# Later steps, row buffers taken twice and own PSUM banks in the projection stages of an attention-and-FFN kernel

## The chip, the core and the metric

The kernel runs on one core of a Trainium2 chip. The core has a matrix engine (TensorE, PE in the profile), a vector engine (VectorE, DVE), a scalar engine (ScalarE, ACT), a general engine (GpSimd, POOL) and a sync engine (SyncE, SP) that here does nothing but issue DMAs. Each engine runs its own instructions in the order of the program and waits on semaphores for the others. The metric is the device time of one execution in microseconds; lower is better. The kernel before takes 2465.11 us (median of 3 runs, 2461.74 to 2465.53).

## What is computed

Eight sequences of 512 rows and 1024 columns in float32 go through one transformer block without learned norms:

```python
x = x + _layernorm(attn(_layernorm(x), Wq, Wk, Wv, Wo))
x = x + _layernorm(ffn(_layernorm(x), weight, bias, lora_A, lora_B, lora_start_indices))
```

`attn` is causal attention with 16 heads of 64 and rotary positions, and ends with a product by `Wo`. `ffn` is one product by a 1024 x 1024 weight plus bias, and for most sequences a rank-16 LoRA term. So each sequence has two large 512 x 1024 by 1024 x 1024 products behind the attention, each followed by a layernorm over rows and an addition of the row that went in. In this text these are the projections: 0 to 7 are by `Wo` (one per sequence), 8 to 15 by the FFN weight.

## The kernel before

The program has three parts: the value projections with the layernorm of the input, then scores and attention, and last the sixteen projections. Only the last part changes, and in it mainly projections 0 to 7. It starts 1.67 ms into the span.

A projection is a Strassen-Winograd product, twice nested: 7 groups (`GROUPS`, order P1, P2, P4, P5, P7, P6, P3) of 7 products each (`SLOTS`, order P6, P1, P3, P5, P4, P7, P2). One product is two 128 x 128 by 128 x 256 matmuls, four records in the profile. So a projection is 49 products, and the program counts them: tick `49*q + 7*g + p` is product p of group g of projection q. `run(tick, filler)` issues the product, then the adds that drain the product before it, then whatever `at(tick, ...)` has put on that tick. Ticks only set the order in each engine's queue; no engine waits for a tick.

A group has four PSUM accumulators. a and b take two products each and have two buffers. c and d are the two halves of one 2 KB bank, also with two buffers; c takes P5 and, two products into the next group, P3, and d takes P4. `Group.drain` empties them: after P1, ACT copies a to `p1` and DVE makes `u2 = p1 + b`; after P7, DVE adds b into `p1` and writes `p1 + d` and `p1 + c` to the result; after P2, ACT copies a out; after P3, DVE writes `c + u2`. Three of these are waits for PE: P7 adds into b, so it waits for `u2`; P3 adds into c, so it waits until the drain after P7 has read c; P2 adds into a, so it waits for the copy to `p1`.

The seven group results are combined by 128 x 1024 additions: on DVE `c11 += A` (tick 18), `U += A` (45), `c22 += U` (46), `c12 += c22` (48), `c22 += A` (52), and on POOL in two halves `c21 += c12` (38), `c21 += U` (47) (line 360). The right operands of the next projection are R11, R21, R12, R22, loaded by SP at ticks 10, 17, 24, 31, and differences T1, T2, T4, T3 of them, which POOL makes at ticks 38, 45, 52 and 63 in three instructions each (line 274). They are written into buffers of the projection that is running: T1 takes the one that held R12, or rather T3, which overwrites R12 in place. T3 is the right operand of group P7, whose last product (P3) is at tick 37.

While projection q+1 runs, the four row tiles t of projection q are finished (`plan_rows`). A row tile is 128 rows by 1024 columns in two halves. For projections 0 to 7 the steps are: load the row of the input (SP), statistics (two `bn_stats`, `bn_aggr`, a square root on ACT, then reciprocal and bias on DVE; key `o`), normalise (two ACT instructions), add the row (two POOL instructions, line 1158), store to `x1`, statistics again (key `x`), normalise into the row's buffer (ACT), transpose in 32 x 32 blocks back into the result's place (two DVE instructions, line 1167), store to `x1t` (eight DMAs, line 1174). Tile t begins at tick `k = 55 + 7*t` of projection q, that is `6 + 7*t` of the next. The row's buffer is held from the load to the transposes; three buffers rotate and one tile of each projection takes a fourth.

Projections 8 to 15 load their right operands from `x1t` (four DMAs each, line 254), take differences of them on POOL and DVE (line 262), have T1 and T3 made by DVE, and have two small LoRA products (line 1187) at ticks 25 and 39 of the projection before. Their row tiles stop after the first addition.

Of the kernel before, what the change touches and what calls it, by code (L numbers as in the profile page):

```python
# [10 lines left out]
F32 = mybir.dt.float32  # L11
# [6 lines left out]
P = 128  # L18
B, S, E = 8, 512, 1024
# [44 lines left out]
SUB = 256  # L64
# [68 lines left out]
def sandwich_kernel(  # L133
# [58 lines left out]
    def at(tick, fn, kind=None):  # L192
        events[tick].append((kind, fn) if kind else fn)
# [100 lines left out]
    class Group:  # L294
# [9 lines left out]
        def product(self, p):  # L304
            l, r, a = SUBS[p]
            first = a not in self.acc
            if a in "ab" and first:
                self.acc[a] = env["acc"].tile([P, SUB], F32, tag=a, bufs=2, name=f"acc{a}_{self.name}")
            elif a == "c" and first:
                both = env["acc"].tile([P, 2, SUB], F32, tag="c", bufs=2, name=f"accc_{self.name}")  # L310
                self.acc["c"], self.acc["d"] = both[:, 0], both[:, 1]
            acc = self.acc[a]
            left, right = self.W[self.L], RX[self.q, self.R][:, SLOT_R[r]]
            for k in range(2):
                stays = right[:, k, :] if self.q < B else by_blocks(right, k)
                if self.q < 0:
                    moving = left[:, SLOT_L[l], k, :]
                else:
                    moving = left[:, 4 * k : 4 * k + 4, SLOT_L[l], :]
                nc.tensor.matmul(  # L320
                    acc, lhsT=stays, rhs=moving,
                    start=(first and k == 0), stop=True, skip_group_check=True,
                )
            if self.lora and p in LORA_SUB:
                half, cols = self.lora
                i, c = LORA_SUB[p]
                nc.tensor.matmul(  # L327
                    acc, lhsT=hts[self.q - B][:, cols[c], :],
                    rhs=env["lb"][self.q - B][:, half * HALF + i * SUB : half * HALF + (i + 1) * SUB],
                    start=False, stop=True, skip_group_check=True,  # L330
                )
# [7 lines left out]
        def drain(self, p):  # L339

            acc, t = self.acc, self.t
            add = lambda out, x, a: nc.vector.tensor_tensor(out, acc[a], x, op=ALU.add)
            if p == "P1":
                env["u2"].reverse()
                for n, pool in (("p1", env["p1"]), ("u2", env["u2"][0])):
                    t[n] = pool.tile([P, SUB], F32, tag=n, name=f"{n}_{self.name}")
                nc.scalar.copy(t["p1"], acc["a"])  # L347
                add(t["u2"], t["p1"], "b")
            elif p == "P7":
                add(t["p1"], t["p1"], "b")  # L350
                add(self.dest(1, 0), t["p1"], "d")
                add(self.dest(1, 1), t["p1"], "c")
            elif p == "P2":
                nc.scalar.copy(self.dest(0, 0), acc["a"])
            elif p == "P3":
                add(self.dest(0, 1), t["u2"], "c")
# [38 lines left out]
    def stats(key, srcs, step):  # L395
        small = env["small"]
        if step == 0:
            ln[key] = small.tile([P, 2, 6], F32, tag="bnst", name=f"bn_{key}")
        if step < 2:
            nc.vector.bn_stats(ln[key][:, step, :], srcs[step])  # L400
        if step == 1:
            mv = small.tile([P, 2], F32, tag="mv", name=f"mv_{key}")
            nc.vector.bn_aggr(mv, ln[key])
            ln[key] = mv
        if step == 2:
            mv = ln[key]
            sd = small.tile([P, 1], F32, tag="sd", name=f"sd_{key}")
            nc.scalar.activation(sd, mv[:, 1:2], AF.Sqrt, bias=eps, scale=1.0)
            ln[key] = mv, sd
        if step == 3:  # L410
            mv, sd = ln[key]
            rs = small.tile([P, 1], F32, tag="rstd", name=f"rstd_{key}")
            nc.vector.reciprocal(rs, sd)
            nb = small.tile([P, 1], F32, tag="nb", name=f"nb_{key}")
            nc.vector.tensor_scalar(nb, mv[:, 0:1], rs, -1.0, op0=ALU.mult, op1=ALU.mult)
            ln[key] = rs, nb
# [683 lines left out]
    with ExitStack() as a:  # L1100
# [23 lines left out]
        def pick_b(b):  # L1124
            lb[b] = (rows if b % 2 else lc).tile([P, E], F32, tag="lb", bufs=1, name=f"lb_{b}")
            pick(lb[b], lora_b, 1, b)
# [12 lines left out]
        def halves(q, t):  # L1139
            h, j = divmod(t, 2)  # L1140
            tags = (("c11", "c21"), ("c12", "c22") if q + 1 == NQ else ("c22", "c12"))[h]
            return [C[q, tag][:, j, :] for tag in tags]

        row = {}

        def load_row(q, t):
            if (q, t) == (NQ - 1, 3):
                row[q, t] = lc.tile([P, E], F32, tag="lb", bufs=1, name=f"row_{q}_{t}")
            elif q < B and t == (3 if q + 1 < B else 0):
                row[q, t] = rows.tile([P, E], F32, tag="lb", bufs=1, name=f"row_{q}_{t}")  # L1150
            else:
                row[q, t] = rows.tile([P, E], F32, tag="row", bufs=3, name=f"row_{q}_{t}")
            src = x[q, ts(t, P), :] if q < B else x1d[q - B][:, t, :]
            nc.sync.dma_start(out=row[q, t], in_=src)

# [45 lines left out]
        def plan_right(q, base):  # L1201

            if q > 1:
                at(base + 6, next_roles)
            for n, k in (("R11", 10), ("R21", 17), ("R12", 24), ("R22", 31)):
                if q == 1 and n != "R22":
                    continue
                at(base + k, lambda n=n: load_right(gp, q, n))
                if q >= B:
                    at(base + k + 4, lambda n=n: sub_right(q, n, nc.gpsimd, slice(0, 3)))  # L1210
            if q >= B:
                for h, k in ((0, 25), (1, 39)):
                    at(base + k, lambda h=h: lora_in(q - B, h), "pe")
                    at(base + k, lambda ph, h=h: lora_keep(q - B, h, ph), "post")
                    for g in range(2):
                        at(base + k, lambda n=f"R{g + 1}{h + 1}": sub_right(q, n, nc.vector if h else nc.gpsimd, slice(3, 4)))
                at(base + 42, lambda: sub_ht(q - B))
                if q - B:
                    at(base + (10 if q - B > 1 else 33), lambda: pick_b(q - B))
                if q + 1 < NQ:  # L1220
                    at(base + 43, lambda: pick_a(q - B + 1))
            for n, k in (("T1", 40 if q == 1 or q >= B else 38), ("T2", 46 if q >= B else 45), ("T4", 52), ("T3", 63)):
                eng = nc.vector if q >= B and n in ("T1", "T3") else nc.gpsimd
                for m in range(3):
                    at(
                        base + k + (m if eng is nc.vector else 0),
                        lambda n=n, m=m, eng=eng: sum_right(gp, q, n, eng, slice(m, m + 1)),
                    )
# [8 lines left out]
        def plan_rows(q, base):  # L1237

            for t in range(NT):
                k = base + 55 + 7 * t  # L1240
                key = f"{'o' if q < B else 'y'}{q}_{t}"
                at(k, lambda t=t: load_row(q, t))
                for m in range(4):
                    at(k + m + m // 2, lambda t=t, m=m, key=key: stats(key, halves(q, t), m))
                for h in range(2):
                    at(k + 6 + h, lambda t=t, h=h, key=key: norm(key, halves(q, t)[h], halves(q, t)[h]))
                    at(k + 8 + h, lambda t=t, h=h: add_row(q, t, h))
                at(k + 14, lambda t=t: store_rows(q, t))
                if q < B:
                    key = f"x{q}_{t}"  # L1250
                    for m in range(4):
                        at(k + 14 + m + m // 2, lambda t=t, m=m, key=key: stats(key, halves(q, t), m))
                    for h in range(2):
                        at(k + 20 + h, lambda t=t, h=h, key=key: norm(
                            key, row[q, t][:, ts(h, HALF)], halves(q, t)[h]
                        ))
                    for g in range(2):
                        at(k + 24 + g, lambda t=t, g=g: turn_x1(q, t, g))
                        at(k + 29 + g, lambda t=t, g=g: store_x1(q, t, g))

        def plan_last(q, base):

# [169 lines left out]
```

## Time and profile before

The profiled execution took 2465.22 us, of which 2463.1 us are the profile's span. All times of places below are microseconds from the span's start.

| part of the span | us | PE busy | DVE busy | POOL busy |
|---|---|---|---|---|
| whole span | 2463.1 | 2352.0 | 1752.8 | 1535.6 |
| while projection 2 runs (1741.28 to 1786.27) | 44.99 | 42.72 | 40.17 | 36.80 |
| while projection 3 runs (1786.27 to 1831.29) | 45.02 | 42.73 | 40.23 | 36.87 |
| while projection 5 runs (1876.30 to 1922.80) | 46.50 | 44.25 | 40.17 | 36.03 |
| while projection 7 runs (1967.82 to 2023.45) | 55.63 | 46.76 | 48.75 | 46.67 |
| while projection 8 runs (2023.45 to 2085.11) | 61.66 | 54.87 | 50.30 | 41.71 |

A stretch is counted from the start of one product P3 at tick 2 to the next, because PE waits there in each of them. PE is the engine with least idle time, so a stretch is read as PE's busy time plus the waits that ended last. The order of the instructions is fixed on every engine, so a late instruction makes all behind it in its queue late too.

### The profile page before, as it was taken

The page shows a single profiled execution, that of the slowest core. Times are in us where ns is not written, and L with a number is a line of the kernel's source. Part 1 is how long each engine was busy: PE and PEld are TensorE (multiplying, and loading weights), DVE is VectorE, ACT ScalarE, POOL GpSimd, SP SyncE. Part 2 cuts the span into 40 slices and gives each one's busy share as a digit, 9 for nine tenths or more (in the row PEclk, how much of TensorE's full clock was granted, in tenths as well). Part 3 has the DMA queues.
Part 4 walks back from the last instruction along what each step waited for, and adds up shares of the span by engine and source line. Part 5 has one row for each costly group of instructions (what it writes and reads, how often), then busy time and mean ns, then how long its engine had stood idle before and what let it go on. Part 6 is the DMA issues. An engine that isn't in the chain of part 4 may idle for free.

```text
span 2463.1 us, 37159 instructions
## 1 busy us (share of the span) xinstructions
PE 2352.0 (95%) x11936; PEld 1857.2 (75%) x11936; DVE 1752.8 (71%) x3834; ACT 1110.5 (45%) x2790; POOL 1535.6 (62%) x1139
## 2 busy tenths in 40 slices
PE   6999999999999999999999999899999988999997
PEld 4888887877677777777777767458888867888886
DVE  8666566475857759586684866776888988777676
ACT  5445541126555555655555566652434333222223
POOL 4978774204463553736645364776886886777874
PEclk8999999999999999999999999999999999999999
DMA  7688887998899897989989896567777798455443
GB/s 277 201 289 263 252 277 250 331 289 270 261 298 281 248 343 238 320 295 291 327 262 333 265 307 232 145 240 262 231 208 241 208 267 237 139 144 146 136 122 120
DMA packets 506017, 606.48 MB, mean 246 GB/s; under 512 B 197600, under 2 KB 344032, under 8 KB 503264
## 3 DMA queue, kind: packets, MB, share of 16 engines
q1 hardware_dynamic: 504288, 598.87, 76.7%
q0 software_dynamic: 1536, 5.24, 0.7%
q8 instruction: 96, 1.57, 0.3%
q14 instruction: 97, 0.79, 0.1%
HBM read 371.20 MB, written 199.23 MB: 232 GB/s over the span
## 4 chain that ended last, share of the span: by engine, by line
PE 69%; DVE 7%; DMA 3%; ACT 2%; POOL 2%; SPq 1%; issue 1%; ACTq 0%; DVEq 0%; POOLq 0%
PE accc_P L320 10%; PE accc_q_P L675 7%; PE accb_q_P L675 7%; PE acca_q_P L675 7%; PE s L787 6%; PE accb_P L320 6%; PE acca_P L320 6%; PE po L869 6%; PE ptp L848 5%; PE accd_q_P L675 4%; DMA R<-x1t 1%; PE accc_P L327 1%; DVE U L360 1%; ACT pr L818 1%; DMA qk<-D_q 1%
## 5 line engine op out<-in xcount | busy, mean ns | idle before, releaser
L818 ACT ACTIVATE pr<-pr,nm 128x128 f32<-128x128 f32 (+3 forms) x512 | 281.0, 550 | 189.1 <-DVE nm L808 189.0
L834 ACT ACTIVATE pr<-pr,rs 128x128 f32<-128x128 f32 x470 | 231.0, 550 | 105.9 <-DVE rs L826 105.8
L808 DVE CUSTOM_DVE_ANT_0 pr<-s,mask 128x128 f32<-128x128 f32 (+3 forms) x512 | 224.5, 485 | 45.3 <-PE s L787 43.4
L675 PE MATMUL accc_q_P<-xs,ls 128*128 128x256 f32 x896 | 218.4, 387 | 0.0
L675 PE MATMUL acca_q_P<-xs,ls 128*128 128x256 f32 x896 | 217.3, 385 | 0.7 <-issue 0.7
L1158 POOL TENSOR_TENSOR c<-c,row 128x512 f32<-128x512 f32 x120 | 161.6, 1355 | 89.3 <-ACT c L450 83.1
L675 PE MATMUL accb_q_P<-xs,ls 128*128 128x256 f32 x896 | 216.3, 384 | 0.8 <-DVE u_q_P L116 0.8
L675 PEld LDWEIGHTS acca_q_P<-xs,ls 128*128 128x128 f32 x896 | 165.3, 190 | 49.8 <-issue 21.9
L675 PEld LDWEIGHTS accc_q_P<-xs,ls 128*128 128x128 f32 x896 | 166.2, 191 | 48.5 <-issue 22.5
L787 PE MATMUL s<-qk 64*128 64x128 f32 (+3 forms) x1024 | 194.7, 472 | 6.7 <-DVE nm L808 4.8
L675 PEld LDWEIGHTS accb_q_P<-xs,ls 128*128 128x128 f32 x896 | 165.4, 190 | 44.9 <-issue 7.7
L848 PE MATMUL ptp<-ident,pr 128*128 128x128 f32 x1280 | 177.6, 278 | 9.8 <-ACT pr L834 7.3
L601 POOL TENSOR_TENSOR wc_g<-wc_g 128x256 f32<-128x256 f32 (+1 forms) x120 | 130.2, 1103 | 79.5 <-DMA wc_g<-in_wqk_dram 76.2
L274 POOL TENSOR_TENSOR T<-R,T 128x512 f32<-128x512 f32 (+1 forms) x96 | 170.5, 1802 | 13.8 <-PE accc_P L320 9.6
L848 PEld LDWEIGHTS ptp<-ident,pr 128*128 128x128 f32 x1280 | 147.3, 142 | 40.6 <-ACT pr L834 11.2
L869 PE MATMUL po<-pT,v 128*64 128x384 f32 (+3 forms) x1024 | 156.3, 444 | 8.2 <-ACT pT L863 6.1
L869 PEld LDWEIGHTS po<-pT,v 128*64 128x64 f32 x1024 | 71.5, 138 | 100.4 <-issue 66.1
L718 POOL TENSOR_TENSOR B_q<-B_q,m 128x1024 f32<-128x1024 f32 x14 | 33.2, 2369 | 180.8 <-DVE B_q L715 180.7
L787 PEld LDWEIGHTS s<-qk 64*128 64x128 f32 x1024 | 73.6, 186 | 48.8 <-issue 28.9
L675 PE MATMUL accd_q_P<-xs,ls 128*128 128x256 f32 x448 | 108.8, 386 | 0.4 <-DVE p_q_P L116 0.4
L863 DVE COPY pT<-ptp 128x384 f32<-128x384 f32 (+1 forms) x132 | 80.5, 615 | 39.4 <-PE ptp L848 39.4
L347 ACT COPY p_P<-acca_P 128x256 f32<-128x256 f32 x109 | 40.5, 372 | 144.0 <-PE acca_P L320 107.5
(938 smaller groups left out, 5775.1 us busy)
## 6 DMA issues: line engine op xcount, KB each, us to landing
ls<-wqk SPq DMA_DIRECT2D x392, 256.0 KB, 5.0
xs<-xop SPq DMA_DIRECT2D x392, 256.0 KB, 5.2
R<-attn SPq DMA_DIRECT2D x32, 896.0 KB, 5.7
wqk<-wc_g SPq DMA_DIRECT2D x16, 1568.0 KB, 9.5
x<-in_x_dram SPq DMA_DIRECT2D x32, 512.0 KB, 9.8
v<-vd SPq DMA_DIRECT2D x64, 256.0 KB, 5.4
attn<-ops SPq DMA_DIRECT2D x16, 1024.0 KB, 7.7
row<-in_x_dram SPq DMA_DIRECT2D x32, 512.0 KB, 5.1
```

What stands on the lines that cost most here:

```text
L274: eng.tensor_tensor(RX[q, n][:, c], RX[q, x][:, c], RX[q, y][:, c], op=ALU.subtract)
L320: nc.tensor.matmul(acc, lhsT=stays, rhs=moving, start=(first and k == 0), stop=True, skip_group_check=True,)
L601: eng.tensor_tensor(out, x, y, op=op)
L675: nc.tensor.matmul(acc[:, :, w, :], lhsT=ls[:, k, w, :], rhs=xs_[:, :, k, :], start=(first and w == 0 and k == 0), stop=True, skip_group_c ...
L787: nc.tensor.matmul(ps[:, j, at : at + L], lhsT=qT[r, qb], rhs=kT[r, : qb + 1], start=True, stop=True,)
L808: nc.vector.tensor_tensor_reduce(out=v[:, j, :], in0=self.ps[qb][:, j, :], in1=work2["mask"][:, S - L :], scale=-1.0 / HD**0.5, scalar=3.0e38,
L818: nc.scalar.activation(v[:, j, :], v[:, j, :], AF.Exp, bias=nm[:, j : j + 1], scale=-1.0, accum_out=sm[:, j : j + 1],)
L834: nc.scalar.mul(v, v, rs[:, j : j + 1])
L848: nc.tensor.transpose(pt[:, n, :], self.pr[qb][:, j, ts(kb, P)], ident)
L863: copy(self.pT[j][:, : qb + 1, ts(qb, P)], self.pt[j][:, : qb + 1, :])
L869: nc.tensor.matmul(po[j * HD : (j + 1) * HD, kb * P :], lhsT=self.v[:, kb, ts(j, HD)], rhs=self.pT[j][:, kb, kb * P :], start=(kb == 0), s ...
L1158: nc.gpsimd.tensor_tensor(c, c, row[q, t][:, ts(h, HALF)], op=ALU.add)
```

## The change

Four things change in the projections; the number of instructions on every engine stays what it was, and so does what each computes.

- The two halves c and d of the shared bank become tiles of their own: c with two buffers, d with one. The drain after P7 reads c first and d second.
- In projections 0 to 7 the steps of a row tile are moved apart. Counted from k: the row's load from 0 to 5; statistics `o` from 0, 1, 3, 4 to 0, 1, 4, 6; the normalisation from 6 to 9; the addition of the row from 8 to 12; the store from 14 to 16; statistics `x` from 14, 15, 17, 18 to 16, 17, 20, 22; the second normalisation from 20 to 25.
- The transposes leave that grid. They were at 79, 86, 93 and 100 of projection q for the four tiles and are at 84, 91, 103 and 107. In the next projection's ticks: from 30, 37, 44, 51 to 35, 42, 54, 58, so those of the last two tiles stand behind the end of that projection. Their stores follow 5 ticks later as before.
- The row's buffer is taken twice: once for the loaded row, until it is added, and again (`open_row(..., True)`) for the second normalisation. Tile 2 (of projection 7 tile 0) takes the fourth buffer on the second occasion.

One gather of LoRA weights (`pick_b` for sequence 1) moves from tick 33 to 39 of projection 8, since it reuses that fourth buffer.

```diff
-            if a in "ab" and first:
-                self.acc[a] = env["acc"].tile([P, SUB], F32, tag=a, bufs=2, name=f"acc{a}_{self.name}")
+            if first and (a in "ab" or self.q >= 0):
+                self.acc[a] = env["acc"].tile(
+                    [P, SUB], F32, tag=a, bufs=1 if a == "d" else 2, name=f"acc{a}_{self.name}"
+                )
...
-                add(self.dest(1, 0), t["p1"], "d")
-                add(self.dest(1, 1), t["p1"], "c")
+                for half, a in ((0, "d"), (1, "c")) if self.q < 0 else ((1, "c"), (0, "d")):
+                    add(self.dest(1, half), t["p1"], a)
...
+        def open_row(q, t, turned=False):
+            if (q, t) == (NQ - 1, 3):
+                pool, tag, bufs = lc, "lb", 1
+            elif turned and t == (2 if q + 1 < B else 0):
+                pool, tag, bufs = rows, "lb", 1
+            else:
+                pool, tag, bufs = rows, "row", 3
+            row[q, t] = pool.tile([P, E], F32, tag=tag, bufs=bufs, name=f"row_{q}_{t}_{int(turned)}")
...
-                at(k, lambda t=t: load_row(q, t))
-                for m in range(4):
-                    at(k + m + m // 2, lambda t=t, m=m, key=key: stats(key, halves(q, t), m))
+                new = q < B
+                at(k + 5 * new, lambda t=t: load_row(q, t))
+                for m, n in enumerate((0, 1, 4, 6) if new else (0, 1, 3, 4)):
+                    at(k + n, lambda t=t, m=m, key=key: stats(key, halves(q, t), m))
                 for h in range(2):
-                    at(k + 6 + h, lambda t=t, h=h, key=key: norm(key, halves(q, t)[h], halves(q, t)[h]))
-                    at(k + 8 + h, lambda t=t, h=h: add_row(q, t, h))
-                at(k + 14, lambda t=t: store_rows(q, t))
-                if q < B:
+                    at(k + (9 if new else 6) + h, lambda t=t, h=h, key=key: norm(key, halves(q, t)[h], halves(q, t)[h]))
+                    at(k + (12 if new else 8) + h, lambda t=t, h=h: add_row(q, t, h))
+                at(k + (16 if new else 14), lambda t=t: store_rows(q, t))
+                if new:
                     key = f"x{q}_{t}"
-                    for m in range(4):
-                        at(k + 14 + m + m // 2, lambda t=t, m=m, key=key: stats(key, halves(q, t), m))
+                    for m, n in enumerate((16, 17, 20, 22)):
+                        at(k + n, lambda t=t, m=m, key=key: stats(key, halves(q, t), m))
+                    at(k + 25, lambda t=t: open_row(q, t, True))
                     for h in range(2):
-                        at(k + 20 + h, lambda t=t, h=h, key=key: norm(
+                        at(k + 25 + h, lambda t=t, h=h, key=key: norm(
                             key, row[q, t][:, ts(h, HALF)], halves(q, t)[h]
                         ))
+                    turn = base + (84, 91, 103, 107)[t]
                     for g in range(2):
-                        at(k + 24 + g, lambda t=t, g=g: turn_x1(q, t, g))
-                        at(k + 29 + g, lambda t=t, g=g: store_x1(q, t, g))
+                        at(turn + g, lambda t=t, g=g: turn_x1(q, t, g))
+                        at(turn + 5 + g, lambda t=t, g=g: store_x1(q, t, g))
```

More of the change, by code (lines that the diff above doesn't have):

```diff
@@ L1144, in sandwich_kernel @@
         row = {}
-        def load_row(q, t):
[L1147 to L1152, printed above, removed]
+        def open_row(q, t, turned=False):
[6 more added lines that the diff above has]
+            row[q, t] = pool.tile([P, E], F32, tag=tag, bufs=bufs, name=f"row_{q}_{t}_{int(turned)}")
+        def load_row(q, t):
+            open_row(q, t)
             src = x[q, ts(t, P), :] if q < B else x1d[q - B][:, t, :]
@@ L1218, in plan_right @@
                 if q - B:
-                    at(base + (10 if q - B > 1 else 33), lambda: pick_b(q - B))
+                    at(base + (10 if q - B > 1 else 39), lambda: pick_b(q - B))
                 if q + 1 < NQ:
```

## Prediction

> **What bounds the kernel now.** I read the page's engine shares first, then PE's waits in the part that changes, then the busy time of each stretch from one tick-2 wait to the next, then the three engines' instructions in order of time around one such wait.
>
> ```profile
> PE 2352.0 (95%) x11936; PEld 1857.2 (75%) x11936; DVE 1752.8 (71%) x3834; ACT 1110.5 (45%) x2790; POOL 1535.6 (62%) x1139
> ...
> PE accc_P L320 <- DVE A L342: 21.9, 8, 4.5
> PE ph L1187 <- DMA R<-x1t: 4.1, 3, 2.3
> ...
> 1786.27:1831.29 45.02, 42.73 (x196) 37.08 (x197) 40.23 (x89) 18.75 (x38) 36.87 (x25) 1.00 0.74 218
> ...
> 1876.30:1922.80 46.50, 44.25 (x196) 38.33 (x196) 40.17 (x89) 18.64 (x38) 36.03 (x25) 0.96 0.72 212
> ```
>
> PE is busy 95% of the span. In the changed part it loses time at one place per projection: the product P3 at tick 2 waits for DVE's drain of the result A (eight waits, 21.9 us). Six are of 2.25 to 2.29 us, at the ends of projections 1 to 6; those at the ends of 7 and 8 are of 4.54 and 3.69. So 45.02 us are 42.73 of PE and one wait. The third row (columns: length, then busy PE, PEld, DVE, ACT, POOL, then granted clock) is a stretch in which the clock was 0.96: it took 1.48 us more.
>
> The wait that ends projection 3, on PE, DVE and POOL (start, duration, instruction):
>
> ```profile
> 1816.76 1.03 PE L320 MATMUL accc_P<-wo_S,R 128*128 128x256 f32 x4
> ...
> 1825.39 1.03 PE L320 MATMUL accb_P<-wo_S,R 128*128 128x256 f32 x4
> ...
> 1831.29 1.13 PE L320 MATMUL accc_P<-wo_S,R 128*128 128x256 f32 x4 [2.29 <-DVE A L342]
> ...
> 1821.54 1.28 DVE L400 BATCH_NORM_STATS2 bn_x<-c 128x6 f32<-128x512 f32 x2
> ...
> 1823.40 0.42 DVE L342 TENSOR_TENSOR u_P<-accb_P,p_P 128x256 f32<-128x256 f32 x1 [0.34 <-ACT p_P L347]
> 1823.74 0.70 DVE L1167 STREAM_TRANSPOSE c<-row 128x512 f32<-128x512 f32 x1
> ...
> 1825.58 2.32 DVE L360 TENSOR_TENSOR U<-U,A 128x1024 f32<-128x1024 f32 x1
> 1827.94 2.17 DVE L360 TENSOR_TENSOR c<-c,U 128x1024 f32<-128x1024 f32 x1
> ...
> 1830.48 0.76 DVE L342 TENSOR_TENSOR A<-accc_P,p_P 128x256 f32<-128x256 f32 x2
> ...
> 1816.17 2.68 POOL L1158 TENSOR_TENSOR c<-c,row 128x512 f32<-128x512 f32 x2 [4.55 <-ACT c L450]
> 1818.82 4.29 POOL L274 TENSOR_TENSOR T<-R,R 128x512 f32<-128x512 f32 x3
> 1823.09 2.50 POOL L360 TENSOR_TENSOR c<-c,c 128x512 f32<-128x512 f32 x2
> 1825.55 6.23 POOL L274 TENSOR_TENSOR T<-R,T 128x512 f32<-128x512 f32 x3
> ```
>
> PE was ready for P3 at 1829.0. DVE's drain ended at 1831.24 because U += A and c22 += U took 2.32 and 2.17 us. The same instruction takes 1.22 us where POOL is idle (at 1690.19); here DVE and POOL take turns. U += A starts with POOL's T2 (1825.55), ends 1.08 after T2's first instruction; T2's second ends 1.14 after U += A; c22 += U ends 1.07 after that; T2's third ends 1.68 after c22 += U (1831.79). I use these four steps below. Ahead of T2 in POOL's queue stand the row additions of tile 3 (1816.17), T1, and c21 += c12.
>
> **The change, part by part.** All in the frame of projection 3, since the stretches repeat within 0.03 us where the clock is full.
>
> *Own banks, c before d.* The wait ends after the first of the two adds instead of the second: 0.76 - 0.42 = 0.34 us earlier. One buffer for d costs nothing: P4 follows P3 by 1.83 us, d is free 0.34 us after c.
>
> *Row steps later: what POOL does.* The order of POOL's queue changes. Tile 3's two additions move from ticks 35, 36 to 39, 40, behind T1 and c21 += c12 (tick 38). T1 cannot start early: it overwrites the buffer of T3 and waits for the last product of group P7, the one at 1816.76, ended 1817.79. POOL waits 0.08 us behind such a product elsewhere (2132.82 to 2132.90, T2), so T1 starts at 1817.87, only 0.95 earlier than now. Then T1 4.27 (1818.82 to 1823.09) and c21 += c12 2.46 (1823.09 to 1825.55): the additions start at 1824.60, end at 1825.87 and 1827.1 (1.27 each, 1.24 apart), and T2 starts at 1827.07. POOL's idle 4.55 us now lie ahead of T1 and hide nothing.
>
> *What DVE does.* Statistics `x` of tile 3 (ticks 43, 44) read those additions, and the first stands ahead of `u2` of the last group (tick 44) in DVE's queue. From 1821.54 DVE has the transposes of tile 1 and a reciprocal and bias (0.63 + 0.29 + 0.62 by the rows at 1823.74 to 1825.58), is free at 1823.08, and then waits for POOL until 1825.91 (0.04 behind the addition, as at 2003.04). Queued behind: `u2` after one 0.60 statistics step, 1826.51 to 1826.92. P7 of the last group needs `u2`; it was on time at 1825.39, now starts at about 1827.0: a new PE wait of 1.6 us. The second statistics step waits until 1827.14; aggregate +0.71, U drain +0.12, U += A +0.44: 1828.41. That is 1.34 us after T2 starts, 0.1 after its second instruction (1.24) has the turn. So U += A waits for that one (to 1829.57) and ends at 1830.65; T2's third ends at 1832.33, c22 += U at 1833.40; p1 += b starts 0.08 before that, A's first add 0.45 later, 0.42 long: 1834.19. P3 starts 0.05 later, 1834.25, with the 0.34 of the first part already in it.
>
> So each stretch grows by 1834.25 - 1831.29 = 2.96 us; six of them: +17.8. Behind the wait DVE has four transposes (tiles 2 and 3, 4 x 0.63) instead of two; their cover is DVE's idle 1.44 us ahead of p1 += b at 1796.24. It is used up, but they add only 1.26, so DVE is level with PE again there; if they missed by 0.5 us, nothing follows, because `u2` and c are needed 2.6 us after their products.
>
> *Later loads and ACT.* The input row is loaded 5 ticks later (4.3 us); it lands in 5.1 us (median) and is added 7 ticks after its issue, 6.0 us: at nothing. ACT is busy 18.75 of 45 us and its normalisations still lie 3 ticks ahead of each addition: at nothing.
>
> *Clock.* PE, ready for P3 at 1827.0 + 3.61 + 0.1 = 1830.7, would wait 3.5 us. Of six waits of 2.28 one was followed by a reduced clock (1876.30), of the two of 4.54 and 3.69 both (0.97 in the stretch from 2023.45). Bounds: as now, or all six. 3.5 is nearest to 3.69, so I take five more at 1.48: +7.4.
>
> [...]
>
> *Ends of projections 7 and 8.* There T1 is DVE's, and its three instructions stand before the statistics of tile 3, so POOL's delay is covered by some 4.7 us of DVE work (1.75 + 1.26 + 1.71). Of the transposes of tiles 1 and 2 on the way to the wait, two move behind it: -1.26 us each. Against it, 16 stores instead of 8 stand in SP's queue in front of the loads of R21 (tick 17), which the LoRA product at tick 25 waits for already. Counted from PE's wait, the first block is transposed at 4.5; 16 stores at 0.47, four R11 loads at 0.54, L11 0.6 and a row 0.4 make 15.2; R21 is now issued at 13.45 (1981.27 - 1967.82): 1.7 later. Bounds per projection: the wait gone (-4.5), or the load's full 1.7. PE idles later in the same stretch in any case (2.30 and 4.54), which hides a delay, so I take -1.26, twice: -2.5.
>
> *Tail and the rest.* In the last projection P3 waits 1.82 for DVE; c first gives -0.3. The gather at tick 39 waits for a transpose at tick 36: at nothing. Projections 9 to 14 have PE waits of at most 0.6, so nothing to win.
>
> **Sum**, against the profiled execution's own 2465.22 us (0.11 over the median, of no account): 2465.2 + 17.8 + 7.4 - 2.5 - 0.3 = 2487.6; I say 2487. A difference of 0.2%, 4.9 us, is about what a measurement can tell from none.
>
> **The rivals.**
>
> [...]
>
> *Faster.* The additions of tile 3 are done before DVE wants them (1823.08). This needs T1 2.8 us earlier, so that it does not wait for the product at tick 37. Then U += A starts at 1823.08 + 2.2 = 1825.3, T2 at 1823.91 (behind the product at 1822.80). If U += A still meets T2's first instruction, P3 starts at about 1829.3: six times -2.0, one slow clock less, and the other terms: 2465.2 - 12.0 - 1.5 - 2.8 = 2449. For it: POOL has idled 4.55 us in front of those additions. Against: T1's wait is on a buffer, and no later instruction of POOL can pass it.
>
> *No change.* The same, but U += A meets T2's second instruction: P3 at 1831.1, -0.2 a stretch: 2465.2 - 1.2 - 2.8 = 2461, within 0.2%. The banks alone are of this kind: 6 x 0.34 = 2.
>
> **How the numbers follow.** Loss as worked out 0.58 (2475 to 2497), smaller loss 0.22 (2466 to 2477), no change 0.08, faster 0.12. Slower by over 0.2% holds the first and nearly all of the second: 0.79; same 0.09; faster 0.12. The range 2466 to 2497 leaves out the faster case, most of no change and little above; its top is the sum plus 1.7 + 1.26 for each of projections 7 and 8 and some slack for a clock reduced at both waits of a stretch.
>
> **What would show it.** In the changed kernel's profile: POOL's `c<-c,row` of tile 3 behind T1 and `c<-c,c`, ended by no ACT wait; DVE's `bn_x` waiting for POOL L1164 some 2.8 us in each of six stretches; PE waiting at accb for `u_P` (1.6) and at accc for A (3.5); stretches near 48 us, with reduced clock near 49.5. A stretch of 43 us, or no DVE wait for POOL, would prove the central step wrong. The prediction also fails if the loads of R21 become much later than 1.7 us.

## Result and the profile after

The changed kernel takes 2490.97 us (median of 6 runs, 2483.53 to 2498.60), the kernel before on the same chip 2465.32 (6 runs, 2461.66 to 2468.10): 1.0107 times, 95% interval 1.0083 to 1.0131. Slower, as forecast, and 4 us from the 2487 that were predicted. The profiled execution took 2498.60 us (span 2496.5), the slowest of the six; the traces below are compared span against span, 33.4 us apart.

PE's waits in the part that changes (us in total, times, longest), to be held against `accc` 21.9, `ph` 4.1 of before:

```profile
PE accc_P L322 <- DVE A L344: 30.1, 8, 4.9
PE accb_P L322 <- DVE u_P L344: 12.6, 8, 2.1
PE ph L1193 <- DMA R<-x1t: 8.4, 4, 3.9
```

The same stretches, from one tick-2 P3 to the next (length, then busy PE, PEld, DVE, ACT, POOL, then granted clock):

```profile
1697.20:1745.19 47.99, 41.49 (x191) 35.56 (x189) 36.64 (x79) 17.86 (x36) 41.58 (x29) 1.00 0.60 200
1745.19:1794.67 49.48, 44.53 (x197) 38.26 (x197) 39.70 (x89) 18.46 (x38) 36.43 (x25) 0.95 0.65 202
1794.67:1845.62 50.95, 45.56 (x197) 39.03 (x197) 41.29 (x89) 18.59 (x38) 35.77 (x25) 0.94 0.63 197
...
1945.47:1993.29 47.82, 42.85 (x197) 37.08 (x197) 39.60 (x89) 18.47 (x38) 35.89 (x25) 1.00 0.67 209
1993.29:2055.13 61.84, 49.51 (x229) 39.90 (x229) 49.65 (x98) 18.68 (x38) 44.24 (x37) 0.93 0.85 256
2055.13:2120.54 65.41, 55.56 (x259) 46.19 (x259) 54.60 (x101) 18.68 (x38) 42.81 (x35) 0.97 0.81 232
```

A stretch that took 45.0 us takes 47.8 where the clock is full, and 49.2 to 51 where it is not. PE's busy time goes with the clock, since the matmuls are the same (42.85 us at a granted clock of 1.00, 44.53 at 0.95, 45.56 at 0.94); what is left of a stretch is waiting. That splits the 33.4 us (before's stretches in the same manner, each part rounded):

| part of the span | more, us | waiting | clock |
|---|---|---|---|
| up to the first of these products (1697.20) | 1.0 | | |
| six steady stretches (1697.20 to 1993.29) | 24.5 | 16.5 | 8.0 |
| stretches of projections 7 and 8 | 10.0 | 6.5 | 3.4 |
| behind them | -2.0 | | |

The wait that ends projection 3, on PE, DVE and POOL (start, duration, instruction):

```profile
1838.30 1.13 PE L322 MATMUL accb_P<-wo_S,R 128*128 128x256 f32 x4 [1.87 <-DVE u_P L344]
...
1845.54 2.07 PE L322 MATMUL accc_P<-wo_S,R 128*128 128x256 f32 x4 [3.52 <-DVE A L344]
...
1837.23 0.70 DVE L402 BATCH_NORM_STATS2 bn_x<-c 128x6 f32<-128x512 f32 x1 [3.19 <-POOL c L1164]
1837.84 0.41 DVE L344 TENSOR_TENSOR u_P<-accb_P,p_P 128x256 f32<-128x256 f32 x1
1838.45 0.69 DVE L402 BATCH_NORM_STATS2 bn_x<-c 128x6 f32<-128x512 f32 x1 [0.21 <-POOL c L1164]
...
1839.71 2.24 DVE L362 TENSOR_TENSOR U<-U,A 128x1024 f32<-128x1024 f32 x1
1841.99 2.71 DVE L362 TENSOR_TENSOR c<-c,U 128x1024 f32<-128x1024 f32 x1
...
1845.06 0.42 DVE L344 TENSOR_TENSOR A<-accc_P,p_P 128x256 f32<-128x256 f32 x1
1845.40 0.41 DVE L344 TENSOR_TENSOR A<-accd_P,p_P 128x256 f32<-128x256 f32 x1
...
1826.76 2.51 POOL L1164 TENSOR_TENSOR c<-c,row 128x512 f32<-128x512 f32 x2 [3.39 <-DMA x<-c]
1829.22 4.28 POOL L274 TENSOR_TENSOR T<-R,R 128x512 f32<-128x512 f32 x3
1833.47 2.51 POOL L362 TENSOR_TENSOR c<-c,c 128x512 f32<-128x512 f32 x2
1835.92 2.50 POOL L1164 TENSOR_TENSOR c<-c,row 128x512 f32<-128x512 f32 x2
1838.36 5.25 POOL L274 TENSOR_TENSOR T<-R,T 128x512 f32<-128x512 f32 x3
```

Read it from POOL: tile 3's additions (1835.92) stand behind T1 and `c21 += c12`; the statistics on DVE wait 3.19 us for them, `u_P` stands behind the statistics, and PE waits at accb. U += A then comes 1.35 us after T2's start, while T2's second instruction runs, and takes 2.24 us; P3 starts 0.06 us after the add that reads c, while d is still being read. One thing was not foreseen: the additions of tile 2 (1826.76) were late too. In this stretch T1 starts at their end, 0.56 us behind the product it waits for (1827.63 + 1.03), and PE's wait at accb is 1.87; in the others T1 starts 0.13 or 0.14 behind that product and the wait is 1.43 to 1.45. So two things stood at T1 at nearly the same moment, the product and a late row, and which mattered was left to the experiments.

### The profile page after: what moved, and what is told of

It reads as the page before. It is cut to its first block, busy times and chain, and to the rows that moved or that the text cites. A ratio compares the mean times of both kernels' runs of the same rounds, so it can differ in the third digit from the quotient of the medians.

```text
span 2496.5 us, 37147 instructions
## 1 busy us (share of the span) xinstructions
PE 2363.3 (95%) x11936; PEld 1866.8 (75%) x11936; DVE 1761.6 (71%) x3834; ACT 1107.8 (44%) x2790; POOL 1530.1 (61%) x1139
## 4 chain that ended last, share of the span: by engine, by line
PE 69%; DVE 6%; DMA 3%; ACT 2%; POOL 1%; SPq 1%; issue 1%; ACTq 0%; DVEq 0%; POOLq 0%
PE accb_q_P L677 7%; PE accc_q_P L677 7%; PE acca_q_P L677 7%; PE accc_P L322 7%; PE accb_P L322 6%; PE acca_P L322 6%; PE s L789 6%; PE po L871 6%; PE ptp L850 5%; PE accd_q_P L677 4%; PE accd_P L322 3%; DVE U L362 1%; DVE c L362 1%; ACT pr L820 1%; DMA wf_L<-wf_d 1%
## 5 line engine op out<-in xcount | busy, mean ns | idle before, releaser
L677 PEld LDWEIGHTS acca_q_P<-xs,ls 128*128 128x128 f32 x896 | 165.3, 190 | 49.8 <-issue 20.6
L274 POOL TENSOR_TENSOR T<-R,T 128x512 f32<-128x512 f32 (+1 forms) x96 | 165.4, 1749 | 14.1 <-PE accc_P L322 9.7
```

The costliest lines, as they stand in the source:

```text
L274: eng.tensor_tensor(RX[q, n][:, c], RX[q, x][:, c], RX[q, y][:, c], op=ALU.subtract)
L677: nc.tensor.matmul(acc[:, :, w, :], lhsT=ls[:, k, w, :], rhs=xs_[:, :, k, :], start=(first and w == 0 and k == 0), stop=True, skip_group_c ...
```

## The experiments

The theory: POOL's order (the additions of tile 3 behind T1) costs the steady stretches their time; own banks gain 0.34 us a wait; the late transposes are harmless there. The rivals: late row loads, a cost of the banks, a cost of the late transposes. Projections 7 and 8, which had been forecast 2.5 us shorter and were 10 longer, were a question of their own: the first guess was the sixteen stores ahead of R21. Each label stands for one kernel.

**Additions ahead of T1.** In the changed kernel:

```diff
-at(k + (12 if new else 8) + h, lambda t=t, h=h: add_row(q, t, h))
+at(k + (10 if t == 3 else 12 + h) if new else k + 8 + h, lambda t=t, h=h: add_row(q, t, h))
```

> The changed kernel, with the two row additions of tile 3 put on tick 37 instead of 39 and 40: ahead of T1 and c21 += c12 in POOL's queue; nothing else moves. Theory (POOL's order is the cause): DVE's 3.19 us wait for POOL before the statistics of tile 3 and PE's 1.45 us wait at accb are gone in all six steady stretches, the wait at accc falls from 3.52 to 1 to 2 us, and a stretch at full clock falls from 47.8 to 43.5 to 45: 2464 to 2471 us in all. Rival (the row loads are late: tile 3's row is issued at 1824.26 and lands about 6.8 us later): POOL waits some 2 us for the row at its additions, T1, T2 and T4 behind them get later, and a new PE wait for T appears; stretches of 45 to 47, 2472 to 2482 us. Rival (own banks cost the time): no change, 2488 to 2494 us.

2479.04 us (1.0041 of before, 1.0019 to 1.0063), 12 less than the changed kernel. DVE's wait for POOL and PE's wait at accb are gone from the boundary, accc is down from 3.52 to 1.0 to 2.2: the theory's mechanism. But behind the first stretch (44.4), the three at full clock take 46.5 to 48.4, not 43.5 to 45; the rival of the late row had said 45 to 47. These stretches, and two POOL lines and a PE line of this kernel:

```profile
1788.40:1834.90 46.50, 43.10 (x196) 37.05 (x196) 40.09 (x89) 18.47 (x38) 35.50 (x24) 1.00 0.71 216
1834.90:1883.31 48.41, 43.10 (x196) 37.03 (x196) 40.77 (x89) 18.47 (x38) 37.97 (x26) 1.00 0.67 206
1883.31:1930.61 47.30, 43.11 (x196) 37.03 (x196) 40.88 (x89) 18.47 (x38) 36.74 (x25) 1.00 0.69 212
...
1825.26 2.50 POOL L1164 TENSOR_TENSOR c<-c,row 128x512 f32<-128x512 f32 x2 [4.24 <-DMA row<-in_x_dram]
1827.72 5.26 POOL L274 TENSOR_TENSOR T<-R,R 128x512 f32<-128x512 f32 x3
...
1849.39 1.13 PE L322 MATMUL accb_P<-wo_L,T 128*128 128x256 f32 x4 [1.93 <-POOL T L274]
```

POOL now idles for tile 3's row, T1 and all behind it are late, and PE waits 1.92 to 1.94 us for a T in each stretch. It also waits at accb just behind the boundary, 0.43 us and in the longest stretch 1.66.

**Row loads at the old tick.** In the changed kernel, alone, and then together with the edit above (the second label):

```diff
-at(k + 5 * new, lambda t=t: load_row(q, t))
+at(k, lambda t=t: load_row(q, t))
```

> The changed kernel, with the row loads put back to tick k (five ticks earlier); everything else as changed. Theory (T1 waits for the last product of P7's group, and the additions stand behind it): POOL's waits for the row at the additions of tiles 1 and 2 (5.73 and 3.39 us) shrink, but T1 starts where it did, DVE's wait for POOL and both PE waits stay, steady stretches stay at 47.6 to 48 at full clock: 2486 to 2493 us. Rival (late row loads, which push T1 back): a stretch shrinks by 1 to 3 us, 2472 to 2484 us.

2490.82 us: no change, and a stretch at full clock is 47.79, against 47.82 without the edit. POOL and PE:

```profile
1824.11 4.28 POOL L274 TENSOR_TENSOR T<-R,R 128x512 f32<-128x512 f32 x3 [4.57 <-PE accc_P L322]
...
1840.43 1.13 PE L322 MATMUL accc_P<-wo_S,R 128*128 128x256 f32 x4 [3.52 <-DVE A L344]
```

The row is no longer what POOL waits for; T1 waits for PE's product, idle for 4.57 us, and P3 follows T1's start by 16.32 us in both kernels. So the wait on T3's buffer, as forecast, sets T1 here, and the late row alone costs nothing.

> The changed kernel with both edits of before, each of which left something: the additions of tile 3 on tick 37 (ahead of T1), and the row loads at tick k. Theory (with the additions first, the late row was what made T1, T2 and T4 late and brought PE's new wait of 1.93 us for T): POOL's additions of tile 3 no longer wait for the row, the wait for T is gone or under 0.5, accc waits 0.5 to 2: stretches of 43.3 to 44.8 at full clock, 2465 to 2474 us. Rival (T is late because two additions more stand ahead of T1, row or no row): wait for T stays at 1.5 to 2, stretches of 46.4, 2474 to 2482 us.

2456.31 us (0.9969, 0.9948 to 0.9991), faster than the kernel before. Tile 3's second addition now waits 0.45 us for ACT and none for a row, T1 starts at 1811.38, 10.9 us ahead of P3, and of PE's waits for T (14.0 us in eight with the additions alone) 2.9 are left, one of 1.54 among them ahead of the steady stretches. A steady stretch:

```profile
1778.15:1822.42 44.27, 42.84 (x197) 37.08 (x198) 39.56 (x89) 18.47 (x38) 36.90 (x25) 1.00 0.72 227
```

Together the two small edits take 3.5 us from each stretch. Alone, the row loads take nothing, and the additions leave the stretches at full clock between 1.3 shorter and 0.6 longer. The time is below the range given: no steady stretch of this profile has a reduced clock, and it reached the projections 6.3 us earlier than the profile of before.

**Old row steps, late transposes.** The changed kernel with the row steps on their old ticks, the late transposes kept for projections 0 to 5, banks and row buffers kept:

```diff
-new = q < B
+new = False
...
-turn = base + (84, 91, 103, 107)[t]
+turn = base + ((84, 91, 103, 107)[t] if q + 2 < B else 79 + 7 * t)
```

> The changed kernel with the row steps back on the old ticks (load to second normalisation, additions of tile 3 ahead of T1) and, for projections 0 to 5, the late transposes kept; for projections 6 and 7 the old transposes too; banks and row buffers as changed. Theory (the later row additions cost the time, later transposes and own banks each gain): in the steady stretches U += A starts some 1.3 us earlier than before, DVE waits for no addition, PE's wait at accc is 0 to 1.5 us instead of 2.28: stretches of 42.9 to 44.4, 2449 to 2460 us. Rival (the late transposes cost time by themselves, four of them behind the boundary and their stores ahead of the row loads): new waits at accb or for T behind the boundary, stretches over 45, 2465 us or more.

2450.52 us (0.9949, 0.9933 to 0.9966), the fastest of this study. PE's wait at accc is at most 1.26 us, and a stretch is

```profile
1780.45:1824.19 43.74, 42.58 (x198) 37.16 (x197) 39.97 (x89) 18.96 (x38) 35.50 (x25) 1.00 0.73 229
```

So three of the four parts of the change are together a gain of 1.3 us a stretch against before, and the moved row steps undo it and 2.8 more. No wait for `u_P` is left in the steady stretches, and one wait of 1.45 for a T.

**The banks.** Alone in the kernel before (two runs), the order alone, and the changed kernel without them:

```diff
-if a in "ab" and first:
-    self.acc[a] = env["acc"].tile([P, SUB], F32, tag=a, bufs=2, ...)
+if first and (a in "ab" or self.q >= 0):
+    self.acc[a] = env["acc"].tile([P, SUB], F32, tag=a, bufs=1 if a == "d" else 2, ...)
...
-add(self.dest(1, 0), t["p1"], "d")
-add(self.dest(1, 1), t["p1"], "c")
+for half, a in ((0, "d"), (1, "c")) if self.q < 0 else ((1, "c"), (0, "d")):
+    add(self.dest(1, half), t["p1"], a)
```

> The kernel before, with only the own banks for c and d and c drained first. Theory (banks are a small gain): each of the eight waits for A is 0.34 us shorter, PE waits at accc 1.9 us in the six steady stretches, stretches of 44.7: 2461 to 2463 us. Rival (one buffer for d or the other order costs time): new waits at accd, stretches of 46 or more, 2470 us or more.

2459.98 us (0.9968, 0.9955 to 0.9981). The six waits are 1.92 to 1.94 and a stretch at full clock 44.66, as forecast; the total gained 7.3 us, not 2.

> The kernel before with only the order of the two last adds of the drain after P7 swapped, c first; c and d stay halves of one bank. Theory (the gain of the bank part is the order, not the banks): PE's waits at accc 1.93 in the six steady stretches as with own banks, 2459 to 2464 us. Rival (the bank itself matters: PE may not write c while d in the same bank is being read, or each drain is slower there): waits of 2.2 or more, 2464 to 2470 us.

2463.38 us (0.9994, 0.9980 to 1.0009), waits of 2.25 to 2.29: the order alone gains nothing. This kernel's drain and P3, and then those of the banks alone:

```profile
1827.99 0.76 DVE L342 TENSOR_TENSOR A<-accc_P,p_P 128x256 f32<-128x256 f32 x2
...
1828.81 1.13 PE L320 MATMUL accc_P<-wo_S,R 128*128 128x256 f32 x4 [2.25 <-DVE A L342]
```

```profile
1826.03 0.42 DVE L344 TENSOR_TENSOR A<-accc_P,p_P 128x256 f32<-128x256 f32 x1
1826.37 0.42 DVE L344 TENSOR_TENSOR A<-accd_P,p_P 128x256 f32<-128x256 f32 x1
...
1826.51 1.13 PE L322 MATMUL accc_P<-wo_S,R 128*128 128x256 f32 x4 [1.92 <-DVE A L344]
```

With one tile for both halves P3 starts 0.06 us after the second read, with two 0.06 after the first. That fits a wait on both reads where the two halves are one tile of the program; whether the bank itself would hold PE back is not shown.

> The kernel with the banks alone once more, in five rounds. Theory (of its 7.3 us some 2 are the shorter waits, the rest lies ahead of the projections, where the two programs are the same, and differs between runs): the six waits are 1.92 to 1.94 again, the time is 2458 to 2465 us, and the first wait of the projections comes anywhere from 1 us later to 7 us earlier than in the profile before. Rival (own banks make the whole kernel faster): 2457 to 2461 us, and the first wait again 6 to 7 us earlier.

2457.16 us (0.9963, 0.9949 to 0.9977): the gain repeats, 8.2 us. Waits 1.92 or 1.93. The product at which the first of the six stretches begins comes 5.2 us earlier than in the profile of before (6.6 in the first run), and up to there the two programs differ only in projection 0.

> The changed kernel with the bank part alone undone: c and d halves of one bank again, d drained first. Theory (the banks are worth 0.34 at each wait for A): PE waits at accc 3.8 to 3.9 instead of 3.52, stretches of 48.1 at full clock, 2492 to 2496 us. Rival (the 7 us of the banks alone belong to them whole): 2496 to 2501 us.

2502.61 us, 1.0147 of before against 1.0107 with banks: some 10 us. The waits are 3.85, 0.33 more, as forecast; the total goes with the rival.

So each of the three says that the banks are worth 7 to 10 us, and the waits named in the forecast are 2 of it. Projections 9 to 15 give another 1.1 to 2.0: there PE has waits of 0.2 to 0.8 for the drain of U, and 1.82 at the very end; with own banks the first are fewer and the last is 1.48 or 1.49. The rest is not settled. The twelve profiled experiments, with own banks or without, reach that first stretch 0.7 to 7.5 us earlier than the profile of before, the changed kernel's own 1.0 later; so the front part, nearly the same in all, varies by itself. Why the medians would follow the banks is open.

**Projections 7 and 8.** First R21 ahead of the stores, in the changed kernel:

```diff
-at(base + k, lambda n=n: load_right(gp, q, n))
+at(base + (9 if n == "R21" and q in (B, B + 1) else k), lambda n=n: load_right(gp, q, n))
```

> The changed kernel, with the loads of R21 of projections 8 and 9 moved from tick 17 to tick 9 of the projections 7 and 8, ahead of the stores of tiles 2 and 3. Theory (sixteen stores in SP's queue ahead of R21 make projections 7 and 8 longer): R21 is issued some 6 us earlier, PE's wait of 3.92 us for R at the first LoRA product of projection 7 falls below 1 us, that of 1.60 in projection 8 to nothing, and the two stretches get 2 to 5 us shorter together; the steady stretches do not change: 2485 to 2489 us. Rival (those waits only move: the products behind them wait for R12's loads or for DVE instead): lora wait at the second product longer by as much, 2490 to 2493 us.

2506.36 us (1.0162, 1.0124 to 1.0200): 15 us more than the changed kernel, a miss. The first LoRA wait fell to 1.55, but R21's first load stood at the head of SP's queue for 16.1 us, until PE had read the buffer's old content 13.3 us into projection 7, and everything behind it stood too: R11 was issued at 17.6 instead of 7.1, tile 0's row so late that POOL waited 6.38 for it, DVE 13.13 for POOL, and PE 8.22 at accb. The steady stretches, which this edit does not touch, repeat those of the changed kernel:

```profile
1740.46:1789.95 49.49, 44.52 (x196) 38.22 (x196) 39.76 (x89) 18.48 (x38) 36.00 (x25) 0.97 0.65 202
1789.95:1837.73 47.78, 42.84 (x196) 37.08 (x196) 39.57 (x89) 18.48 (x38) 35.87 (x25) 1.00 0.67 210
```

**Old steps and transposes for the rows of projections 6 and 7 only**, the changed kernel elsewhere (`new = q + 2 < B`, and the transposes as above):

> The changed kernel with all steps, transposes and stores of the rows of projections 6 and 7 (they are finished while 7 and 8 run) back on the old ticks; projections 0 to 5 as changed. Theory (what the changed kernel lost in projections 7 and 8 comes from its later steps and from sixteen stores ahead of the loads in SP's queue): projection 7 back from 61.8 to 55 to 57 us, 8 from 65.4 to 61 to 64, the steady stretches unchanged at 47.8 at full clock: 2480 to 2486 us. Rival (those two projections are longer by the clock or by the banks alone): 2488 us or more.

2488.99 us: the rival's number. Projections 7 and 8 take 59.6 and 65.7, in which PE waits 20.7 us together, against 22.2 in the changed kernel and 15.7 before. Putting these rows back gave little. The wait for R21 (3.84) stayed, since the last two tiles of projection 5 still store at the start of projection 7. One profile each says little here, though: the kernel with the old row steps has the same program in projection 8, and PE waits 2.6 us there, against 9.6 in this one.

**L11 late.** L11 is the first block of the FFN weight that SP loads in projection 7. What SP's queue waited for in projection 7 of the changed kernel, and its DMAs there:

```profile
SPq L1180 <- DMA wf_L<-wf_d: 8.2, 2, 4.5
```

```profile
2002.49 0.53 SPq L240 DMA_DIRECT2D wf_L<-wf_d  x1
2003.12 2.52 SPq L1180 DMA_DIRECT2D x1t<-c  x4
2005.68 0.43 SPq L1160 DMA_DIRECT2D row<-in_x_dram  x1
2006.21 7.53 SPq L1180 DMA_DIRECT2D x1t<-c  x8
2013.85 2.06 SPq L254 DMA_DIRECT2D R<-x1t  x4
```

Eight stores take 7.53 us instead of some 3.8, because the third of them stands 3.7 us. It is the eighth DMA after L11 (1.8 MB; such loads take 8.5 to 10.7 us to landing in this stretch). The trace names L11 as what it waited for, and the later weight loads are waited for too (4.2 and 1.7 us in the kernel of the next edit). In the traces of the kernel before and of the changed one, six DMAs of SP's queue wait 1.5 to 4.5 us for a load of the FFN weight, and each is the eighth behind it; what holds it there is not shown. So L11 goes behind R12 and R22:

```diff
-("L11", "L12", "L22", ...), (10, 22, 34, ...)
+("L11", "L12", "L22", ...), (32, 22, 34, ...)
```

> The changed kernel with the load of L11 (1.8 MB, tick 10 of projection 7, in SP's queue ahead of the last twelve stores) moved to tick 32. Theory (the eighth DMA that SP issues after L11, a store of tile 3, waits 4.0 us until L11 has landed, and the loads of R21 stand behind it): the stall in SP's queue and PE's wait of 3.92 us at the first LoRA product of projection 7 are gone or under 0.8, projection 7 takes 56 to 59.5 us instead of 61.8, nothing else moves: 2484 to 2489 us. Rival (the DMAs themselves are slow there, 0.85 of their time busy): R21 is issued earlier but lands no earlier, the wait stays over 2 us, or the second LoRA product waits longer by as much: 2490 us or more.

```profile
1982.22:2033.09 50.87, 46.05 (x229) 37.81 (x230) 44.20 (x98) 18.69 (x38) 40.01 (x34) 1.00 0.84 254
2033.09:2104.64 71.55, 54.94 (x259) 45.68 (x259) 51.96 (x101) 18.57 (x38) 44.99 (x38) 0.93 0.87 254
...
2067.87 1.59 PE L1193 MATMUL ph<-R,la 128*32 128x256 f32 x8 [10.29 <-DMA R<-x1t]
```

2483.98 us, at the lower end of the theory's range, and the eight stores take 3.85 us; R21 is issued 15.6 us into projection 7 instead of 20.6, the first LoRA wait is gone (the second is 2.49), and projection 7 is 11 us shorter, 3.5 of it clock, and 4.8 shorter than in the kernel before. But projection 8 then waits 10.29 us for its own R: the waiting in both together is 21.4 us, against 22.2. The stall is shown, and so is that removing it does not bring back what the two projections lost. They share SP's queue and the weight loads in it, and in this profile the time saved in one is waited for in the other.

> The kernel with the old row steps, late transposes for projections 0 to 5, own banks and row buffers taken twice (2450.5 us), with L11 at tick 32 too. Theory (the same stall of SP's queue): its wait of 3.85 us at the first LoRA product of projection 7 goes, 2444 to 2448 us. Rival (projection 7 then waits for DVE or POOL at the same place or at its end): 2449 us or more.

2457.11 us, 6.6 more than without this edit: a miss in the same way (6.86 us wait for R in projection 8).

## Why the prediction was right, by its own steps

**Six stretches x 2.96.** Measured 2.78 (47.78 to 47.80 against 45.01 at full clock, seven times in the two kernels with R21 early and with the old last two, whose steady part is the changed kernel's) and 2.93 for the first: 16.8 us against 17.8. The two numbers on PE were 1.43 to 1.45 at accb (predicted 1.6; 1.87 once) and 3.52 at accc (3.5). The margin of 0.1 us by which U += A comes behind T2's second instruction held every time (0.10 to 0.12 us in the six stretches). That POOL's order is the cause is shown by the additions moved ahead of T1: both waits change at once, and with the rows on time the stretch falls from 47.79 to 44.27 by that edit alone. That T1 is held by the product at tick 37 is shown by the early row loads, which by themselves change nothing.

**Later loads "at nothing".** Right for this kernel, and for a wrong reason: the rows do come late, POOL idles 5.73 and 3.39 us for those of tiles 1 and 2, but T1 could not have started sooner. With the additions ahead of T1, the same loads cost 2.2 to 4.1 us a stretch (46.5 to 48.4 against 44.3). A cover was named that hides the loads only while something else is later.

**Own banks, 0.34 a wait.** 0.33 to 0.35 in all three comparisons. "Nothing to win" in projections 9 to 14 and 0.3 at the tail missed 0.8 to 1.7 us; 3 to 5 us more of the banks' worth are unexplained.

**Clock, +7.4.** 8.0 in the profiled execution, but that was partly luck. Between the first of the waits at accc and the last there are five stretches per profile; counted by PE's busy time, they had a reduced clock in 4, 4, 1, 1 and 3 of 5 in the five profiled kernels with waits of 3.52 us, in 5 of 5 with 3.85, in 8 of 25 in the five whose longest waits are 1.9 to 2.3, and in none of 15 in the three with waits of at most 1.45. "All six" should have been about half of them, +3 us instead of +7.4, with a spread of its own (what it goes with stands in the last section): that is also where the changed kernel's spread of 15 us may come from, against 6 of before.

**Ends of projections 7 and 8, -2.5.** The failed step: +10.0, of which 3.4 clock. Two of its terms were wrong. R21's loads came 7.1 us later, not 1.7 (20.56 against 13.45 us into projection 7): the stores were counted at 0.47 us each with no wait among them, and one of them waits 3.7 us for L11. PE's wait at the first LoRA product is 3.92 us for it, against 0.15 before. And the drains were to come 1.26 earlier in each, but PE waits 4.93 and 4.07 us for A there, against 4.54 and 3.69. What makes the two together wait 5 to 6 us more than before remains open. Neither the old steps of their rows, nor R21 early, nor L11 late brought it back. The old row steps throughout did (14.0 us of waits), with R21 as late (20.5 us) and the wait for it as long (3.85), and so did the additions ahead of T1 (16.2), but not together with early rows (20.6). With 7 us between two kernels whose programs are the same in projection 8, single profiles do not settle it.

**The sum and the rivals.** Against the profiled execution the sum was 11.0 us short: 12.5 in projections 7 and 8 and 1.0 ahead of the steady stretches, less 0.7 in these and 1.7 behind (rounded). That the median is only 4 us off is owed to that execution being the slowest of its six. Rival "faster" described what happens when T1 does not stand ahead of the additions: it gave 2449 us, and the kernel with the old row steps measured 2450.5. That kernel gets there with the old order of the additions, own banks and late transposes, and not by the rival's earlier T1, so the nearness of the two numbers is partly luck.

## What to carry to other kernels

When a step is moved later, look in each engine's queue at what it now stands behind, and at what that waits for; here two 1.3 us additions, four ticks later, cost 3.5 us in every stretch (47.8 against 44.3 with the rows on time), by a wait of the instruction that they were put behind. Price a load as hidden only together with the reason why nobody could use it sooner: two harmless delays may hide each other, and removing either alone shows little (on average 0.4 and 0 us a stretch here, 3.5 for both). Count SP's DMA queue among the engines: here a load moved to its front moved its wait of 16.1 us onto all behind it (R11 was issued at 17.6 instead of 7.1).

## What the runs showed of the hardware

Moving the wait from one projection to the next left the sum of waits where it was (22.2 and 21.4 us), with the DMA engines busy 0.81 to 0.87 of the time. That was not expected.

In the trace of the changed kernel the granted clock falls to 0.50 in pieces of 3.4 or 6.8 us (1745.52 to 1748.93 is one, with 1.00 in the 3.41 us on either side). At the ends of the steady stretches they start at whole multiples of 3.41 us from each other (1745.5, 1793.3, 1844.5, 1895.7: 14, 15 and 15 times). The same wait of 3.52 us comes with one in four places and without in two, and which of the two goes with where it lies on this grid. In the profiles of the kernel before and of the changed one, from 1690 to 2130 us, all 11 starts of reduced clock (3 and 8) lie on such a grid, each profile on its own. In the eleven pieces of 3.41 us that end at these starts PE's waits come to 2.1 to 3.1 us; in no other piece of the two grids at full clock do they come to more than 1.93. The wait that ends at 1945.40 is cut by the grid at 1943.5 into 1.6 and 1.9, and the clock stays at 1.00. A stretch of 47.79 us is 14.0 such pieces, and the next wait is cut into 1.6 and 1.9 again, and again the clock stays; with R21 early four stretches in a row, of 47.78 or 47.79 us, keep the full clock.

U += A takes 1.23 us where POOL is idle (at 1690.19 in the kernel before) and 2.24 when it meets T2's second instruction (at 1839.71 in the changed one), but 5.44 and 5.45 at the ends of projections 7 and 8, where it starts 0.10 us ahead of T2 and yet ends 1.1 us after all three of its instructions (2047.51 to 2052.95 against 2047.61 to 2051.85): the forecast let the two engines take turns, and there they did not. It was so before too (4.12 and 4.14 us, started 1.23 behind T2 and ended 1.09 behind its end), so the order of the starts does not explain it; why is open.
